# A row-recurrent LSTM after a group normalisation: residual addition to GpSimd three half-steps late, the shared third's normalisation to ScalarE, and a new order in the steady loop

## The chip, the cores and the metric

One Trainium2 chip, one of its cores. The metric is the device time of one execution in microseconds (us), median of several runs. Engines are called as in the profile: PE is TensorE, DVE is VectorE, ACT is ScalarE, POOL is GpSimd, SP is SyncE, which issues all DMAs here.

## The reference

All is float32. `x` is 8 images of 96 channels, 128 rows, 128 columns. It is normalised in 32 groups of three channels; a masked 1x3 convolution makes four gates' inputs for every pixel; then an LSTM runs down the 128 rows, one row at a time, its state passing through a 1x3 convolution along the row; the states are added to `x`.

```python
its = conv(gn(x), W_is * mask) + b_is          # 384 gate rows for each pixel
def step(carry, row_in):
    h, c = carry
    ss = conv1d(h, W_ss) + b_ss                # three taps along the row
    f, i, o, g = split(ss + row_in)            # sigmoid, sigmoid, sigmoid, tanh
    c_new = f * c + i * g
    h_new = o * tanh(c_new)
    return (h_new, c_new), h_new
out = x + scan(step, rows of its)
```

## The kernel before

The rows depend on each other, so the kernel has little else to overlap than two halves of the batch. A half-step is one row of one half (`s`, four images): 96 channels on partitions, 512 pixels along them, even pixels first (`t=0`, 256), then odd ones. `place(n)` gives half-step `n` its row and half: even `n` are half 0, a row ahead. Half-steps 2 to 253 are written by one string of names, `PERIOD`, that `do` plays once for each `n`; the engines then run their instructions in just that order (`manual_schedule`), each waiting on semaphores. A mark behind a name moves it to another half-step: `'` one back, `''` two, `'''` three, `+` one on. `<` and `>` choose the upper or lower 64 rows of TensorE, which work side by side.

The three-tap convolution is done by products of sums and differences. From the new state in `hx` four operands are made: `S` (`total`, L670, `vs`, even plus odd) and `F` (`difference`, L674, `vf`) on DVE, `D0` (`shifted_even`, L680, `te`) and `D1` (`shifted_odd`, L684, `vo`) on POOL. `te` needs only the even pixels of the state, `vo` only the odd ones. The 384 gate rows lie in three PSUM banks of 128 rows: A (forget gate, and 32 rows of g), B (input gate, and 32 rows of o), C (64 rows of o, 64 of g). In each bank products 1 and 2 (with `vs` and `vf`) are made first. ACT copies half of the bank out (`cp`, L583), DVE adds and subtracts (`lo` L587, `hi` L591), and only then products 0 and 3 (with `vo`, `te`) and the products of the input, `P`, `Q` and `E`, are added to the same bank. In the chain of waits, `loC` and `hiC` are the last pair of a half-step, right behind `S` in DVE's queue.

Then come the gates. ACT: `si` (sigmoids, L615; L618 is `o2`, the 32 rows of o in bank B), `ta` (tanh of g, L596), `th` (tanh of the cell, L650, odd pixels then even). DVE: `fg` (f*c, L623), `gtb` (i*g of the odd pixels, L632), `ceb` and `cea` (the cell, L642), `oub` and `oua` (the state, L658). POOL: `gta` (i*g of the even pixels, L630).

Beside the recurrence, POOL prepares later rows: `widen` (L337, `xw`) normalises an image's 64 channels, `add_pixels` (L354) and `subtract_pixels` (L358, `xs`) make the input's operands. In `PERIOD` these are `W1`, `W2` and `W3`. The other 32 channels ("the shared third") share the partitions 96 to 127 of the state's tiles: `normalise_shared` writes them into `hx`, by ACT (L335) where the part is a single row, named `X`, and by POOL (L337, `hx`) otherwise, named `U`. Over four rows each half has four parts of four, four, four and three rows, and one part of one row.

`residual` (`re`) adds the state to the `x` tile in place, on DVE (L700), one half-step behind; then `finish` lets SP store a block of four rows (L703) and, when the store has landed, load the block after next into the same tile (L182, L183).

Of the kernel before, what the change touches and what calls it, by code (L numbers as in the profile page):

```python
# [21 lines left out]
def kernel(  # L22
# [29 lines left out]
    nc = tc.nc  # L52
# [365 lines left out]
    NT = NB * R  # L418
# [3 lines left out]
    def place(n):  # L422

        row, s = divmod(n, NH)
        return row + (LEAD if s == 0 else 0), s
# [50 lines left out]
    class HalfStep:  # L476
# [158 lines left out]
        def part(self, ap, lo, hi, t=None):  # L635
            ap = ap.rearrange("p (t b j) -> p t b j", t=2, b=BH)
            return ap[:, :, lo:hi] if t is None else ap[:, t, lo:hi]
# [52 lines left out]
        def residual(self, lo=0, hi=BH, t=None):  # L690
            s, row = self.s, self.row
            if t is not None:
                xo = xt[s, row // R][0:C, :, row % R, :].rearrange("p b (j t) -> p t b j", t=2)
                nc.vector.tensor_add(xo[:, t], xo[:, t], self.h[:, t])
                return
            xo = xt[s, row // R][0:C, :, row % R, :].rearrange("p b (j t) -> p t b j", t=2)
            if self.n < 1:
                nc.gpsimd.tensor_add(xo, xo, self.h)
            else:
                nc.vector.tensor_add(xo, xo, self.h)  # L700

    def store(s, k, lo, hi):
        nc.sync.dma_start(  # L703
# [40 lines left out]
    def work(n):  # L744
        row, s = place(n)
        if row >= NT:
            return [], (), []
        if n < len(FIRST):
            return FIRST[n]
        k, r = divmod(row, R)  # L750
        ahead, image = (k + 2, 0) if r == R - 1 else (k + 1, r + 1)
        return (
            shared(s, k + 1, *SHARED[r]) if k + 1 < NB else [],
            own(s, ahead, image) if ahead < NB else (),
            ([LATER[n]] if n in LATER else [])
            + ([(spare, s, k + 1)] if r == R - 2 and k + 1 < NB else [])
            + ([(load_rows, s, k + 2)] + ([(load, 0, k + 2)] if s == 1 else [])
               if r == R - 2 and k + 2 < NB else []),
        )
# [3 lines left out]
    def prepare(n, which="123"):  # L763

        channels, image, rest = worked.setdefault(n, [list(parts) for parts in work(n)])
        now = []
        for name, engine in (("X", nc.scalar), ("U", nc.gpsimd)):
            if name in which:
                now += [part for part in channels if part[1] is engine]
                channels[:] = [part for part in channels if part[1] is not engine]  # L770
        for i in "123":
            if i in which and int(i) <= len(image) and image[int(i) - 1]:
                now.append(image[int(i) - 1])
                image[int(i) - 1] = None
        if image.count(None) == len(image) and n not in closed:
            closed.add(n)
            now += rest
        for part, *args in now:
            part(*args)
# [3 lines left out]
    def finish(n):  # L783
        prepare(n)
        row, s = place(n)
        k, r = divmod(row, R)
        if r == R - 1:
            store(s, k, R - 1 if k + 1 == NB else 0, R)
            if s == 1 and k + 2 < NB:
                load(s, k + 2)  # L790
        elif r == R - 2 and k + 1 == NB:
            store(s, k, 0, R - 1)
# [2 lines left out]


    PERIOD = (
        "2B> siA' cpB 2A< siBb' 0C'> 1A< cpA fg' D0'' 3C'> QC< loB QA+> taCb' 1C< hiB PB+> 2C< "
# [3 lines left out]
    )  # L802
    LAST = (
        "2B'' 2A'' 1B'' 1A'' cpB'' cpA'' loB'' 1C'' hiB'' 2C'' loA'' EB'' hiA'' 0B'' 3A'' 0A'' "
        "3B'' cpC'' loC'' EA'' taA'' hiC'' 0C'' 3C'' PA QA PB QB PC QC EA EB siBa'' siA'' siBb'' "
        "fg'' taCb'' taCa'' gtb'' siC'' gta'' ceb'' cea'' o2'' thb'' oub'' tha'' oua'' F'' S'' "
        "D1'' D0'' re'' 1A 2A 1B 1C 2B 2C cpA loA hiA cpB loB 3A hiB 0A 0B 3B cpC loC hiC 0C 3C "
        "taA siA fg o2 siBa siBb taCa taCb gta gtb siC ceb cea thb tha oub oua reb rea"
    )
# [12 lines left out]
    def half_step(n):  # L822
        if n not in steps:
            steps[n] = HalfStep(n)
        return steps[n]

    def do(n, names, by_lanes=False):

        for name in names.split():
            if name in "UX":  # L830
                prepare(n - NH, name)
                continue
            if name[0] == "W":
                prepare(n - 1 + name.count("+") - name.count("'"), name.strip("W+'"))
                continue
            at = n
            for mark, offset in (("'", -1), ("+", 1), ("*", 2)):
                at += offset * name.count(mark)
                name = name.replace(mark, "")
            images = None  # L840
            lane = "<>".find(name[-1]) if name[-1] in "<>" else None
            name = name.rstrip("<>")
            if name[0] in OWN and name[-1] in IMAGES:
                images, full = IMAGES[name[-1]], name[:-1]
            else:
                full = name
            pixels = PIXELS[name[-1]] if name[:-1] in SPLIT and name[-1] in PIXELS else ()
            whole_name = name[:-1] if pixels else full
            tile_ = whole_name[-1] if whole_name[-1] in order else ""
            part = whole_name[: len(whole_name) - len(tile_)]  # L850

            if part in ("S", "F", "D0", "D1"):
                at += NH
            if place(at)[0] >= NT:
                continue
            step = half_step(at)
            if name in step.done or whole_name in step.done:
                continue
            if by_lanes and (part in OWN or part in H_PRODUCTS) and (
                n < last or part in ("P", "Q") or (part, order[tile_]) in step.halves  # L860
            ):
                if step.piece(part, order[tile_], images, lane):
                    step.done.add(name)
                continue
            step.done.add(name)
            getattr(step, PARTS[part])(*([order[tile_]] if tile_ else []), *pixels)
            if by_lanes and part == "re" and at < last:
                finish(at)
# [55 lines left out]
    def next_products():  # L924


        late[0:0] = [Scale(1, 0, BH - 1)]
        late.insert(1, Scale(1, BH - 1, BH, late[0].banks))
        for a in range(2):
            half_step(1).take_bank(a)  # L930
        do(2, "PA PB QA QB PC QC 1A 2A 1B 2B 1C 2C")
# [19 lines left out]
    def keep_warm(count):  # L951
        if not early_done and 1 not in steps:
# [30 lines left out]
        at(4, 10): lambda: (  # L983
            spare_rows(0, 0, 1),
            do(-2, "PA PB QA QB PC QC EA EB"),
        ),
        at(4, 15): lambda: (
            do(-2, "1A 2A 1B 2B 1C 2C"),
            do(-2, "cpA"),
            do(-2, "cpB"),  # L990
# [125 lines left out]
    for b in range(B):  # L1116
# [7 lines left out]
        for k in range(QW // CH):  # L1124
# [11 lines left out]
            if alone:  # L1136
                i = list(shares).index(k)
                part = slice(0, alone * SN) if k % 2 else slice(CH - alone * SN, CH)
# [131 lines left out]
```

## Time and profile before

| | |
|---|---|
| median of 3 runs | 2147.67 us (2146.77 to 2148.72) |
| the profiled execution | 2147.14 us; span of its records 2145.3 us |
| busy: PE, DVE, ACT, POOL | 95%, 86%, 74%, 74% of the span |
| granted TensorE clock | 0.995 of full speed |
| L700 `residual` on DVE | 253 times, 918 ns in the mean, 680 ns at the least |
| L337 `hx`, shared third on POOL | 185 times 869 ns, 60 times 752 ns |
| L335 `hx`, shared third on ACT (one row) | 63 times 493 ns |

How to read it: PE is busy nearly all the time in the records, but a busy record of PE isn't PE at its peak. The steady loop is some 1970 us of the time, so a change of 0.1 us in each half-step is worth 25 us. One query lists instructions by time, with start, duration and, in brackets, the idle time before and what ended it; one follows the chain of work that ended last; one lists least, median and greatest duration of an instruction.

### The profile page before, as it was taken

Reading aid. Unit: us, or ns where it says so; the run is one execution under the profiler, and the core shown is the slowest. Engines: PE = TensorE matmul, PEld = TensorE weight load, DVE = VectorE, ACT = ScalarE, POOL = GpSimd, SP = SyncE. Lnnn points to the kernel's source line nnn. Section 1 sums busy time; section 2 is a strip of 40 time slices with the busy share of each in tenths; the row PEclk is TensorE's granted clock in tenths of the full one; section 3 lists DMA queues with packets and bytes.
Section 4 is the critical chain, followed back from the end, with each engine's and each line's share of the span. In section 5 each row is a group of like instructions: output and inputs, shape, how many; then the busy total and the mean of one; then the engine's idle time right before and its main releaser. Section 6 shows DMA issues by size and latency. Waiting matters only on the chain.

```text
span 2145.3 us, 45095 instructions
## 1 busy us (share of the span) xinstructions
PE 2044.4 (95%) x16400; PEld 1727.8 (81%) x16400; DVE 1841.4 (86%) x4018; ACT 1584.9 (74%) x3519; POOL 1581.3 (74%) x1917
## 2 busy tenths in 40 slices
PE   3689999999999999999999999999999999999998
PEld 0357888888888888888888888888888888888886
DVE  5788888888888888888888888888888888888887
ACT  6687777777777777777777777777777777777776
POOL 4457877777777777777777777777777777777752
PEclk9989999999999999999999999999999999999999
DMA  9973443343344334334433433443343344334311
GB/s 404 412 222 94 99 109 82 95 114 100 84 102 107 84 95 114 99 83 103 107 83 95 114 98 83 104 107 83 95 114 98 83 105 106 83 95 114 92 35 31
DMA packets 110286, 242.79 MB, mean 113 GB/s; under 512 B 6832, under 2 KB 16368, under 8 KB 104048
## 3 DMA queue, kind: packets, MB, share of 16 engines
q1 hardware_dynamic: 110064, 239.89, 42.0%
q8 instruction: 131, 2.15, 0.4%
q14 instruction: 91, 0.75, 0.1%
HBM read 181.34 MB, written 50.33 MB: 108 GB/s over the span
## 4 chain that ended last, share of the span: by engine, by line
DVE 53%; ACT 21%; PE 18%; issue 4%; DMA 2%; POOL 2%; SPq 0%; DVEq 0%; POOLq 0%; ACTq 0%
PE ps L512 18%; DVE ps L591 12%; DVE ps L587 11%; DVE vs L670 9%; ACT ps L650 7%; DVE c L642 7%; ACT m L583 6%; DVE hx L658 5%; DVE vf L674 5%; DVE g L632 3%; ACT g L596 2%; ACT o L618 2%; DMA xs<-in_x_dram 2%; ACT o L615 2%; ACT hx L335 1%
## 5 line engine op out<-in xcount | busy, mean ns | idle before, releaser
L512 PE MATMUL ps<-vo,wl 64*128 64x256 f32 (+1 forms) x3042 | 815.3, 392 | 27.3 <-DVE ps L591 2.1
L512 PE MATMUL ps<-vs,wm 64*128 64x256 f32 (+1 forms) x3046 | 808.2, 397 | 8.4 <-POOL vs L670 6.0
L512 PE MATMUL ps<-vf,wm 64*128 64x256 f32 (+1 forms) x3046 | 794.9, 385 | 3.2 <-DVE vf L674 1.8
L512 PE MATMUL ps<-te,wl 64*128 64x256 f32 (+1 forms) x3042 | 771.7, 377 | 0.0
L512 PE MATMUL ps<-xs,wx 64*128 64x256 f32 (+1 forms) x3080 | 727.7, 377 | 2.0 <-POOL xs L354 1.8
L512 PEld LDWEIGHTS ps<-xs,wx 64*128 64x128 f32 x3080 | 561.4, 187 | 7.4 <-POOL xs L354 3.4
L512 PEld LDWEIGHTS ps<-vo,wl 64*128 64x128 f32 (+1 forms) x3042 | 421.3, 185 | 163.3 <-DVE ps L591 129.4
L512 PEld LDWEIGHTS ps<-vf,wm 64*128 64x128 f32 (+1 forms) x3046 | 492.7, 186 | 71.5 <-DVE vf L674 29.2
L583 ACT ACTIVATE m<-ps,wl 128x256 f32<-128x256 f32 x766 | 363.1, 474 | 235.1 <-PE ps L512 208.9
L596 ACT ACTIVATE g<-ps 32x512 f32<-32x512 f32 x765 | 317.9, 448 | 254.4 <-PE ps L512 247.9
L512 PEld LDWEIGHTS ps<-te,wl 64*128 64x128 f32 (+1 forms) x3042 | 493.0, 187 | 13.3 <-issue 0.2
L512 PEld LDWEIGHTS ps<-vs,wm 64*128 64x128 f32 (+1 forms) x3046 | 424.9, 186 | 67.3 <-DVE vs L670 40.8
L680 POOL TENSOR_TENSOR te<-hx 96x256 f32<-96x256 f32 x254 | 215.4, 848 | 292.8 <-DVE hx L658 290.8
L587 DVE TENSOR_TENSOR ps<-m,ps 128x256 f32<-128x256 f32 x768 | 324.7, 423 | 82.4 <-ACT m L583 82.0
L358 POOL TENSOR_TENSOR xs<-xw 128x512 f32<-128x512 f32 (+1 forms) x254 | 380.5, 1498 | 20.2
L591 DVE TENSOR_TENSOR ps<-m,ps 128x256 f32<-128x256 f32 x768 | 325.8, 425 | 17.6
L658 DVE TENSOR_TENSOR hx<-o,ps 96x256 f32<-96x256 f32 x512 | 197.4, 415 | 130.0 <-ACT ps L650 129.5
L512 PE MATMUL ps<-xs,wt 64*128 64x256 f32 x1012 | 299.4, 376 | 1.5 <-DVE ps L591 1.5
L630 POOL TENSOR_TENSOR g<-i,g 96x256 f32<-96x256 f32 x251 | 182.6, 727 | 123.9 <-ACT g L596 123.9
L615 ACT ACTIVATE ps<-ps 96x512 f32<-96x512 f32 (+1 forms) x512 | 244.0, 477 | 0.2
L700 DVE TENSOR_TENSOR x<-x,hx 96x512 f32<-96x512 f32 x253 | 232.2, 918 | 0.0
L337 POOL TENSOR_SCALAR hx<-x,rstd,nmr 32x512 f32<-32x512 f32 (+1 forms) x245 | 205.8, 840 | 24.7
(118 smaller groups left out, 2524.4 us busy)
## 6 DMA issues: line engine op xcount, KB each, us to landing
xr<-in_x_dram SPq DMA_DIRECT2D x124, 512.0 KB, 6.4
x<-in_x_dram SPq DMA_DIRECT2D x62, 768.0 KB, 5.9
out_dram<-x SPq DMA_DIRECT2D x62, 768.0 KB, 4.7
xs<-in_x_dram SPq DMA_DIRECT2D x31, 1024.0 KB, 11.2
x<-in_x_dram SPq DMA_DIRECT2D x62, 256.0 KB, 3.2
te<-in_x_dram SPq DMA_DIRECT2D x8, 1024.0 KB, 11.3
hx<-in_x_dram SPq DMA_DIRECT2D x8, 1024.0 KB, 9.7
te<-xs SPq DMA_DIRECT2D x62, 128.0 KB, 2.5
```

What stands on the lines that cost most here:

```text
L337: return engine.tensor_scalar(dst, src, scale, shift, ALU.mult, ALU.add)
L358: return engine.tensor_sub(differences, strided(xw[:, 0, :], 0, [(W + 1, n), (J + 1, 2), (1, J)]), strided(xw[:, 0, :], J, [(W + 1, n), (0 ...
L512: made = nc.tensor.matmul(self.ps[a][:, bass.ts(half, HB)][:, cols], weights[rows, bass.ts(a, P)], rhs[rows, cols], start=new, stop=False, ...
L583: nc.scalar.activation(self.m1[a], m1, AF.Identity, bias=column)
L587: nc.vector.tensor_add(self.ps[a][:, 0:HB], self.m1[a], self.ps[a][:, HB:])
L591: nc.vector.tensor_sub(hi, self.m1[a], hi)
L596: nc.scalar.activation(self.part(g, lo, hi, t), self.part(ps, lo, hi, t), AF.Tanh)
L615: nc.scalar.activation(to, gate, AF.Sigmoid)
L658: nc.vector.tensor_mul(self.h[:, t, lo:hi], o, th)
L670: engine.tensor_add(self.operand("vs")[:, 0, lo:hi], e, o)
L680: nc.gpsimd.tensor_sub(to, h[:, :, 1 : J + 1], h[:, :, 0:J])
L700: nc.vector.tensor_add(xo, xo, self.h)
```

## The change

Three edits. `residual` is always given to POOL (L697 in the changed kernel, which is a few lines shorter), and `PERIOD` names it `re'''` instead of `re'`: the state of three half-steps ago. `prepare` now gives the parts of `U` to ACT as well, so that all of the shared third is normalised there. And `PERIOD` and `LAST` have a new order.

```diff
-            if self.n < 1:
-                nc.gpsimd.tensor_add(xo, xo, self.h)
-            else:
-                nc.vector.tensor_add(xo, xo, self.h)
+            nc.gpsimd.tensor_add(xo, xo, self.h)
...
-                now += [part for part in channels if part[1] is engine]
+                now += [
+                    (part[0], nc.scalar, *part[2:]) for part in channels if part[1] is engine
+                ]
...
     PERIOD = (
-        "2B> siA' cpB 2A< siBb' 0C'> 1A< cpA fg' D0'' 3C'> QC< loB QA+> taCb' 1C< hiB PB+> 2C< "
...
+        "2B> 3C'< siBa' D0'' QB+> QC+< 2C> PB+< 1C> loA cpB re''' PC+< hiA 0A> taCb' taCa' loB "
...
-            if place(at)[0] >= NT:
+            if place(at)[0] >= NT or (by_lanes and at < 0):
```

The first place is POOL's queue over one half-step in the middle of the kernel, before: the even operand `te`, the shared third into `hx`, the differences `xs`, the odd operand `vo`, the next image into `xw`, the even product into `g`, the sums `xs`.

```order
L680 TENSOR_TENSOR te0_78<-hx01_71 96x256
L337 TENSOR_SCALAR hx00_70<-x0_16_11221,rstd0_104,nmr0_106 32x4x2x64
L358 TENSOR_TENSOR xs10_76<-xw0_82 128x4x2x64
L684 TENSOR_TENSOR vo_0_63_11758<-hx01_71 128x256
L337 TENSOR_SCALAR xw0_82<-xr0_80,rstd0_104,nmr0_106 128x4x2x64
L630 TENSOR_TENSOR g_1_61_11709<-i_1_61_11723,g_1_61_11709 96x256
L354 TENSOR_TENSOR xs01_75<-xw0_82 128x4x64
```

The same queue now, over as many rows.

```order
L630 TENSOR_TENSOR g_1_61_11600<-i_1_61_11617,g_1_61_11600 96x256
L358 TENSOR_TENSOR xs10_76<-xw0_82 128x4x2x64
L337 TENSOR_SCALAR xw0_82<-xr0_80,rstd0_104,nmr0_106 128x4x2x64
L684 TENSOR_TENSOR vo_1_62_11688<-hx11_73 128x256
L680 TENSOR_TENSOR te1_79<-hx11_73 96x256
L697 TENSOR_TENSOR x0_15_10429<-x0_15_10429,hx01_71 96x2x4x64
L354 TENSOR_TENSOR xs01_75<-xw0_82 128x4x64
```

The shared third is gone from POOL, the residual is new there. Behind the product L630 now stand L358 and L337, and the odd operand L684 comes right behind them and ahead of the even one, L680.

The second place is ACT's queue over one half-step, before, from the copy of bank A of the next half-step to the copy of its bank C, in a half-step whose part `X` is there: `ta`, two sigmoids of o, the two tanhs of the cell and between them the shared third.

```order
L583 ACTIVATE m0_0_73_13514<-ps0_0_73_13434,wl_64 128x256
L596 ACTIVATE g_1_71_13488<-ps2_1_71_13387 64x256 x2
L615 ACTIVATE o_1_71_13535<-ps2_1_71_13387 64x512
L618 ACTIVATE o_1_71_13535<-ps1_1_71_13346 32x512
L650 ACTIVATE ps1_1_71_13346<-c1_85 96x256
L335 ACTIVATE hx01_71<-x0_19_13357,nmr0_106,rstd0_104 32x2x64
L650 ACTIVATE ps2_1_71_13387<-c1_85 96x256
L583 ACTIVATE m2_0_73_13564<-ps2_0_73_13474,wl_64 128x256
```

The same queue now, from the tanh of g in bank A on.

```order
L596 ACTIVATE g_0_67_12390<-ps0_0_67_12280 32x512
L618 ACTIVATE o_0_67_12395<-ps1_0_67_12234 32x512
L583 ACTIVATE m0_1_66_12398<-ps0_1_66_12366,wl_64 128x256
L615 ACTIVATE i_0_67_12407<-ps1_0_67_12234 96x256
L583 ACTIVATE m1_1_66_12419<-ps1_1_66_12324,wl_64 128x256
L596 ACTIVATE g_0_67_12390<-ps2_0_67_12236 64x256 x2
L615 ACTIVATE o_0_67_12395<-ps2_0_67_12236 64x512
L650 ACTIVATE ps1_0_67_12234<-c0_84 96x256
L650 ACTIVATE ps2_0_67_12236<-c0_84 96x256
L335 ACTIVATE hx11_73<-x1_17_12157,nmr1_107,rstd1_105 32x4x2x64
L583 ACTIVATE m2_1_66_12454<-ps2_1_66_12326,wl_64 128x256
```

The sigmoid L618 went from right ahead of the cell's tanhs to ahead of the first copy. The shared third stands behind both tanhs and ahead of the copy of bank C, in each half-step now. The copies L583 come A then B, with one sigmoid between them as before.

The third place is DVE's queue over one half-step from `loC` on, before.

```order
L587 TENSOR_TENSOR ps2_0_69_12762<-m2_0_69_12852,ps2_0_69_12762 128x256
L591 TENSOR_TENSOR ps2_0_69_12762<-m2_0_69_12852,ps2_0_69_12762 128x256
L700 TENSOR_TENSOR x1_16_11454<-x1_16_11454,hx11_73 96x2x4x64
L623 TENSOR_TENSOR ps0_0_69_12722<-ps0_0_69_12722,c0_84 96x512
L587 TENSOR_TENSOR ps1_1_68_12814<-m1_1_68_12886,ps1_1_68_12814 128x256
```

The same now.

```order
L587 TENSOR_TENSOR ps2_0_74_13468<-m2_0_74_13600,ps2_0_74_13468 128x256
L591 TENSOR_TENSOR ps2_0_74_13468<-m2_0_74_13600,ps2_0_74_13468 128x256
L623 TENSOR_TENSOR ps0_0_74_13508<-ps0_0_74_13508,c0_84 96x512
L587 TENSOR_TENSOR ps0_1_73_13598<-m0_1_73_13630,ps0_1_73_13598 128x256
L591 TENSOR_TENSOR ps0_1_73_13598<-m0_1_73_13630,ps0_1_73_13598 128x256
```

The residual is gone; behind `hiC` and `fg` bank A comes ahead of bank B. The rest of DVE's queue has the same instructions in the same order.

More of the change, by code (lines that the diff above doesn't have):

```diff
@@ L797 @@
     PERIOD = (
-        "2B> siA' cpB 2A< siBb' 0C'> 1A< cpA fg' D0'' 3C'> QC< loB QA+> taCb' 1C< hiB PB+> 2C< "
[3 rows of a table removed]
+        "2B> 3C'< siBa' D0'' QB+> QC+< 2C> PB+< 1C> loA cpB re''' PC+< hiA 0A> taCb' taCa' loB "
+        "gtb' 1C< hiB 3A> ceb' 2C< 0B> W2 0A< EB> siC' gta' 3A< 3B> cea' EA< thb' tha' oub' X "
+        "oua' U W3 PA+> cpC 3B< QA+> 0B< F' 2A+> S' 2B+< loC siA siBb W1+ hiC 1A+> 1B+< 0C> 2A+< "
+        "taA D1' 3C> o2 1A+< cpA+ fg 1B+> 0C<"
     )
     LAST = (
-        "2B'' 2A'' 1B'' 1A'' cpB'' cpA'' loB'' 1C'' hiB'' 2C'' loA'' EB'' hiA'' 0B'' 3A'' 0A'' "
-        "3B'' cpC'' loC'' EA'' taA'' hiC'' 0C'' 3C'' PA QA PB QB PC QC EA EB siBa'' siA'' siBb'' "
-        "fg'' taCb'' taCa'' gtb'' siC'' gta'' ceb'' cea'' o2'' thb'' oub'' tha'' oua'' F'' S'' "
+        "re'''' re''' 2A'' 2B'' 1A'' 1B'' cpA'' 2C'' 1C'' loA'' cpB'' hiA'' 0A'' loB'' hiB'' 3A'' 0B'' EB'' "
+        "3B'' EA'' cpC'' loC'' siA'' siBb'' hiC'' 0C'' taA'' 3C'' PA QA PB QB PC QC EA EB o2'' "
+        "fg'' siBa'' taCb'' taCa'' gtb'' ceb'' siC'' gta'' cea'' thb'' tha'' oub'' oua'' F'' S'' "
         "D1'' D0'' re'' 1A 2A 1B 1C 2B 2C cpA loA hiA cpB loB 3A hiB 0A 0B 3B cpC loC hiC 0C 3C "
```

3 rows, old and new, of the table PERIOD are left out of this document.

## The prediction

> **What bounds the kernel now.** I read the page's shares first, then how far apart one instruction of each half-step lies, then the chain of work that ended last, then the queues of ACT, POOL and DVE in order of time.
>
> ```profile
> PE 2044.4 (95%) x16400; PEld 1727.8 (81%) x16400; DVE 1841.4 (86%) x4018; ACT 1584.9 (74%) x3519; POOL 1581.3 (74%) x1917
> ```
> ```profile
> L670 DVE TENSOR_TENSOR vs<-hx x205: 831/834/837, 403.4 to 1999.6; 128x256 f32<-128x256 f32 x103
> ```
>
> 204 half-steps in 1596.2 us: 7.825 us each. The chain shows what they are made of (start, us, what).
>
> ```profile
> 1007.04 0.44 DVE ps L591
> ...
> 1007.52 1.19 PE ps L512 x8
> ...
> 1008.73 0.48 ACT m L583
> ...
> 1011.55 0.43 DVE c L642
> 1011.98 0.68 ACT ps L650 x2
> ...
> 1012.72 0.42 DVE hx L658
> ...
> 1013.16 0.42 DVE vf L674
> 1013.59 0.75 DVE vs L670
> 1014.34 0.35 DVE ps L587
> ...
> 1014.71 0.44 DVE ps L591
> ...
> 1020.05 0.49 ACT hx L335
> ...
> 1020.56 0.39 ACT ps L650
> ...
> 1022.98 0.44 DVE ps L591
> ```
>
> It is one loop per half-step, through all engines. `hiC` (L591) ends at 1007.48 and lets PE go on; four products later (eight records, 1.19) ACT copies a bank, DVE takes it through to the cell (L642), ACT makes the tanhs, DVE the state, F (L674), S (L670), `loC` (L587) and the next `hiC`. From 1007.04 to 1014.71 it is 7.67 us. The next one is 8.27: there ACT's part `X` of the shared third (L335) lies between the two tanhs. Three of one and one of the other make 7.82, as measured. So the residual L700 isn't on the path; DVE does it while PE and ACT turn round.
>
> **Part by part.** I go along this loop.
>
> *The turn-round, 0 to +0.08.* Before, two bank copies with one sigmoid between them; in the new order the same with the banks' names changed. The first starts 1.25 after `hiC`, as before. I take +0.04.
>
> *The tanhs, -0.26.*
>
> ```profile
> 1009.55 0.47 ACT L583 ACTIVATE m<-ps,wl 128x256 f32<-128x256 f32 x1
> 1010.05 0.65 ACT L596 ACTIVATE g<-ps 64x256 f32<-64x256 f32 x2
> ...
> 1011.34 0.59 ACT L618 ACTIVATE o<-ps 32x512 f32<-32x512 f32 x1
> 1011.96 0.69 ACT L650 ACTIVATE ps<-c 96x256 f32<-96x256 f32 x2
> ```
> ```profile
> 1010.78 0.73 POOL L630 TENSOR_TENSOR g<-i,g 96x256 f32<-96x256 f32 x1 [0.34 <-ACT g L596]
> 1011.47 0.73 POOL L354 TENSOR_TENSOR xs<-xw 128x256 f32<-128x256 f32 x1
> 1013.21 0.85 POOL L680 TENSOR_TENSOR te<-hx 96x256 f32<-96x256 f32 x1 [1.01 <-DVE hx L658]
> ```
>
> L596 ends at 1010.70 and the second tanh at 1012.65: 1.95. The first tanh was held by L618 up to 1011.93. With L618 moved ahead of the copies, what stays is POOL's product (starts 0.08 after L596, 0.73), the cell (0.04 and 0.43) and its tanh (0.02 and 0.39): 1.69. That removes 0.26 from each half-step, and in every fourth `X`, 0.60 more, leaves the gap between the tanhs.
>
> *The shared third on ACT: hidden, but for 0.04.*
>
> ```profile
> L700 DVE TENSOR_TENSOR x<-x,hx 96x512 f32<-96x512 f32 x253 | 232.2, 918 | 0.0
> ...
> L335 ACT ACTIVATE hx<-x,nmr,rstd 32x512 f32<-32x512 f32 x7 | 5.9, 843 | 6.9 <-DVE nmr L329 6.7
> ...
> L698 POOL TENSOR_TENSOR x<-x,hx 96x512 f32<-96x512 f32 x2 | 2.6, 1294 | 0.0
> ```
> ```profile
> L337 POOL TENSOR_SCALAR xw<-xr,rstd,nmr x205: 796/808/821, 399.4 to 1995.7; 128x512 f32<-128x512 f32 x103
> ```
>
> It stands between the second tanh and the copy of bank C, for which `loC` waits. After the tanh that takes 0.03 + 0.84 + 0.03 + 0.47 = 1.37, with `X` as well 1.89. `loC` has to wait for S anyway: 0.06 + 0.42 + 0.03 to the start of F, then (next item) 1.31 less an overlap of 0.08, so 1.74. Where `X` is there too, `loC` is 0.17 late, in one half-step of four: 0.04. ACT's work grows from 74% of 7.82 = 5.8 to 6.6 us a half-step, which still fits. If S came earlier, this cover of 0.37 would go first.
>
> *The residual on POOL: no time itself, and 0.92 less on a DVE that wasn't waited for there.* POOL gains 1.29 and loses 0.8; it is busy 5.8 of 7.8 now. L697 stands behind `te`, ahead of the product L630, which waits for ACT anyway.
>
> *F and S against POOL, +0.13: the disputed term.* F and S read two operands in SBUF, and the trace shows such DVE instructions and POOL's as taking turns. Before, POOL was idle when F came; then L680 started 0.05 after F, and S, 0.42 where nothing is beside it, took 0.83, ending 0.28 after L680. F's start to S's end: 1.18. Now L630 waits for the tanh of g, with L358 and L337 right behind it, so POOL is at work when F comes. L630's start to that of its follower is 0.69, L358 takes 1.16, and between L358 and L337 lie 0.11 (below): L337 starts 1.96 after L630. F starts 0.73 + 0.04 + 0.43 + 0.02 + 0.39 + 0.06 + 0.42 + 0.03 = 2.12 after L630. So L337 is 0.16 ahead. POOL first, the prologue:
>
> ```profile
> 162.99 1.16 POOL L358 TENSOR_TENSOR xs<-xw 128x512 f32<-128x512 f32 x1
> 164.26 1.24 POOL L337 TENSOR_SCALAR xw<-xr,rstd,nmr 128x512 f32<-128x512 f32 x1
> ...
> 208.81 0.79 POOL L337 TENSOR_SCALAR xw<-xr,rstd,nmr 128x512 f32<-128x512 f32 x1
> ```
> ```profile
> 164.13 0.42 DVE L674 TENSOR_TENSOR vf<-hx 128x256 f32<-128x256 f32 x1
> 164.47 0.42 DVE L670 TENSOR_TENSOR vs<-hx 128x256 f32<-128x256 f32 x1
> ...
> 209.07 1.08 DVE L700 TENSOR_TENSOR x<-x,hx 96x512 f32<-96x512 f32 x1
> ```
>
> At 164 L337 had started 0.21 ahead of S, and yet S ran in its 0.42 and L337 took 1.24, ending 0.61 after S. At 209 L337 was 0.26 ahead of L700 and went first: L700 took 1.08 instead of its 0.68. So this instruction's start counts for turns only between 0.21 and 0.26 later, and with 0.16 F should still go first. Then L337 waits from before S comes, as L680 did, and goes second: 0.42 + 0.61 + 0.28 = 1.31, +0.13. The bounds are -0.42, if S stays right behind F as at 164 (0.34 + 0.42 = 0.76), and +0.49, if F loses (below).
>
> The Trainium skill (SBUF — State Buffer, "SBUF: two separate sides") says that VectorE and GpSimd share a port pair by an exclusive lock, which whichever of the two starts first keeps for its whole instruction. By the letter of that rule L337 would go first, which is the first rival; S at 164.47 came ahead of an L337 that had started before it, so this trace goes with the lock, but not with the start as printed.
>
> **Sum.** A half-step without `X`: 7.67 + 0.04 - 0.26 + 0.13 = 7.58; with the 0.04, 7.62 in the mean, against 7.825. `PERIOD` writes 252 half-steps, the last four with no image to prepare: 0.205 x 248 = 51 us. The profiled execution took 2147.1 (the median is 2147.7): **2096 us**. About 40 of the 51 come from the half-steps with `X` (8.27 to 7.75, some 62 of them: 32) and 8 or more from the others. Start and end change by little: `LAST` keeps its sequence of products, and a residual of 1.29 there stands ahead of the last row's.
>
> **The rivals.**
>
> *F loses to L337 (slower).* Then F waits out L337 and S the odd operand L684, which now stands ahead of `te`. The last half-steps of this kernel have just that order (POOL: L684, L680):
>
> ```profile
> 2129.62 0.67 DVE L674 TENSOR_TENSOR vf<-hx 128x256 f32<-128x256 f32 x1
> 2130.22 0.83 DVE L670 TENSOR_TENSOR vs<-hx 128x256 f32<-128x256 f32 x1
> ```
> ```profile
> 2129.40 0.62 POOL L684 TENSOR_TENSOR vo<-hx 128x256 f32<-128x256 f32 x1 [1.38 <-DVE hx L658]
> 2129.97 0.80 POOL L680 TENSOR_TENSOR te<-hx 96x256 f32<-96x256 f32 x1
> ```
>
> F ended 0.27 after L684, L680 0.48 after F, S 0.28 after L680. Here: L337's rest 0.80 - 0.16 = 0.64, F 0.27, the POOL operand 0.48, S 0.28: 1.67, +0.49 over 1.18. A half-step is then 7.67 + 0.04 - 0.26 + 0.49 = 7.94, `X` is hidden, +0.115 x 248 = +29: **2176**. It decides where L337's lead passes some 0.21; mine is 0.16 from eight seams read to 0.01 or 0.02. Chance 0.28.
>
> *S stays right behind F (faster still).* The loop falls by 0.55 more, but PE, 95% busy, leaves 5% of 7.825: not under 7.43. 0.39 x 248 = 97: **2050**. Against it: L680 got between F and S in every steady half-step. Chance 0.10.
>
> *The residual's lateness reaches the loads.*
>
> ```profile
> out_dram<-x SPq DMA_DIRECT2D x62, 768.0 KB, 4.7
> ...
> x<-in_x_dram SPq DMA_DIRECT2D x62, 256.0 KB, 3.2
> ```
>
> The block's store comes two half-steps later, and the load of 256 KB, from which ACT makes the shared third, waits for it: 4.7 + 3.2 + 0.1 = 8.0 after the last residual. The first part that reads it comes in the next half-step behind the tanhs, some 10.8 after that residual (7.6, and from about 1.6 to about 4.8 after `hiC`). 2.8 spare; if they were gone, each microsecond costs 62 us, one for each block's load: **2160** with one. Chance 0.05.
>
> *No change* (the gain on the tanhs given back to POOL, about +0.38 in the disputed term): **2143 to 2152**. Chance 0.05. That the change doesn't do what it says is excluded: in the built order L700 and POOL's part of `hx` are gone from the steady loop.
>
> **How the numbers follow.** My case has 0.47: 2096, with 0.08 either way in a half-step 2076 to 2116. Rivals 0.28, 0.10, 0.05, 0.05; 0.05 is left for cases between 2116 and 2143. Faster by over 0.2% (4.3 us, what a measurement of this kernel can just tell): 0.47 + 0.10 + 0.05 = 0.62, and 0.01 for parts of the others: 0.63. Same 0.05. Slower 0.32. The range has to hold my case and the first rival with its own 0.08 upward (2196) and reaches down halfway to the second: 2055 to 2196.
>
> **What would show it.** Right: F at 0.42 and S at about 0.9 in the new trace, L337 `xw` at over 1.1 us, the second tanh ending 1.7 after L596, L335 between tanh and copy with no wait of L587 for L583 but in every fourth half-step. Wrong: F over 0.6 and L337 at 0.81 (first rival); S at 0.42 (second); ACT's L335 waiting for a DMA (third). If L618's move brings less than 0.26, or the first copy starts later than 1.25 after `hiC` because ACT isn't free, the sum fails in that term.

## The result and the profile after

The changed kernel takes 2165.92 us (median of 4, 2164.55 to 2167.02) where the kernel before takes 2147.42 (4 runs) on the same chip: a ratio of 1.0085, 95% interval 1.0068 to 1.0103. It is slower by 18.5 us, inside the range on record but on the other side of no change: the first rival, F losing to L337, is what happened.

The profile after: first the page's busy shares, then the two DVE operands in the steady stretch from 400 to 2000 (least, median and greatest ns).

```profile
PE 2064.0 (95%) x16400; PEld 1716.8 (79%) x16400; DVE 1771.0 (82%) x3765; ACT 1756.3 (81%) x3764; POOL 1589.0 (73%) x1925
```
```profile
L674 DVE TENSOR_TENSOR vf<-hx x202: 608/898/916, 406.1 to 1994.8; 128x256 f32<-128x256 f32 x101
L670 DVE TENSOR_TENSOR vs<-hx x202: 827/829/832, 406.9 to 1995.6; 128x256 f32<-128x256 f32 x101
```

DVE does less than before and ACT more, as the edits say. S starts 202 times from 406.9 to 1995.6: 7.904 each, against 7.825. F takes 0.90 where it took 0.42, and S 0.83 as before. The chain of waits over one half-step (start, us, what):

```profile
1008.83 0.44 DVE ps L591
...
1009.31 1.18 PE ps L512 x8
...
1010.52 0.48 ACT m L583
...
1013.01 0.34 DVE c L642
...
1013.43 0.39 ACT ps L650
...
1013.85 0.39 ACT ps L650
...
1014.26 0.43 DVE hx L658
...
1014.72 0.88 DVE vf L674
1015.60 0.75 DVE vs L670
1016.35 0.35 DVE ps L587
...
1016.72 0.44 DVE ps L591
```

It is the same loop, without L335 in it and without the half-steps of 8.27: the longest from one S to the next is now 8.08. POOL's queue at that time, and ACT's:

```profile
1012.57 0.73 POOL L630 TENSOR_TENSOR g<-i,g 96x256 f32<-96x256 f32 x1 [1.70 <-ACT g L596]
1013.26 1.15 POOL L358 TENSOR_TENSOR xs<-xw 128x512 f32<-128x512 f32 x1
1014.51 0.81 POOL L337 TENSOR_SCALAR xw<-xr,rstd,nmr 128x512 f32<-128x512 f32 x1
1015.28 0.79 POOL L684 TENSOR_TENSOR vo<-hx 128x256 f32<-128x256 f32 x1
1016.03 0.79 POOL L680 TENSOR_TENSOR te<-hx 96x256 f32<-96x256 f32 x1
```
```profile
1011.84 0.65 ACT L596 ACTIVATE g<-ps 64x256 f32<-64x256 f32 x2
...
1014.26 0.73 ACT L335 ACTIVATE hx<-x,nmr,rstd 32x384 f32<-32x384 f32 x1
1015.02 0.48 ACT L583 ACTIVATE m<-ps,wl 128x256 f32<-128x256 f32 x1
```

L337 starts at 1014.51, F at 1014.72. The time by which L337's recorded start is ahead of F's is called its lead from here on. L337 keeps its own 0.81, F ends 0.28 after it, and S 0.28 after L684: so F has waited out L337, and S has waited out L684. From F's start to S's end it is now 1.63, where before it was 1.18. `loC` (L587) comes straight behind S: ACT's copy (ending 1015.50) isn't waited for.

### The profile page after: what moved, and what is told of

It is laid out like the page before. It is cut to its first block, busy times and chain, and to the rows that moved or that the text cites. A ratio compares the mean times of both kernels' runs of the same rounds, so it can differ in the third digit from the quotient of the medians.

```text
span 2165.2 us, 46287 instructions
## 1 busy us (share of the span) xinstructions
PE 2064.0 (95%) x16400; PEld 1716.8 (79%) x16400; DVE 1771.0 (82%) x3765; ACT 1756.3 (81%) x3764; POOL 1589.0 (73%) x1925
## 4 chain that ended last, share of the span: by engine, by line
DVE 59%; PE 17%; ACT 16%; issue 4%; DMA 2%; POOL 1%; ACTq 0%; SPq 0%; DVEq 0%; POOLq 0%
PE ps L512 17%; DVE ps L591 14%; DVE ps L587 13%; DVE vf L674 10%; ACT ps L650 9%; DVE vs L670 9%; ACT m L583 6%; DVE hx L658 5%; DVE g L632 5%; DVE c L642 4%; DMA xs<-in_x_dram 2%; DVE bst L1141 1%; DMA te<-in_x_dram 1%; ACT g L596 0%; POOL xw L337 0%
## 5 line engine op out<-in xcount | busy, mean ns | idle before, releaser
L512 PE MATMUL ps<-vo,wl 64*128 64x256 f32 (+1 forms) x3042 | 889.5, 391 | 27.5 <-DVE ps L591 3.2
L512 PE MATMUL ps<-vf,wm 64*128 64x256 f32 (+1 forms) x3046 | 830.2, 394 | 0.8 <-DVE vf L674 0.8
L512 PE MATMUL ps<-vs,wm 64*128 64x256 f32 (+1 forms) x3046 | 743.3, 395 | 12.1 <-POOL vs L670 8.1
L512 PEld LDWEIGHTS ps<-vo,wl 64*128 64x128 f32 (+1 forms) x3042 | 519.8, 186 | 168.9 <-DVE ps L591 129.6
L583 ACT ACTIVATE m<-ps,wl 128x256 f32<-128x256 f32 x766 | 363.0, 474 | 239.1 <-PE ps L512 212.9
L587 DVE TENSOR_TENSOR ps<-m,ps 128x256 f32<-128x256 f32 x768 | 326.6, 426 | 264.6 <-ACT m L583 264.3
L630 POOL TENSOR_TENSOR g<-i,g 96x256 f32<-96x256 f32 x251 | 182.4, 727 | 441.8 <-ACT g L596 441.8
L512 PEld LDWEIGHTS ps<-vf,wm 64*128 64x128 f32 (+1 forms) x3046 | 444.1, 186 | 17.6 <-DVE vf L674 2.0
L591 DVE TENSOR_TENSOR ps<-m,ps 128x256 f32<-128x256 f32 x768 | 325.6, 424 | 17.5
L697 POOL TENSOR_TENSOR x<-x,hx 96x512 f32<-96x512 f32 x255 | 331.6, 1300 | 0.2 <-DVE hx L658 0.2
L596 ACT ACTIVATE g<-ps 32x512 f32<-32x512 f32 x765 | 317.8, 447 | 13.2 <-PE ps L512 0.9
L358 POOL TENSOR_TENSOR xs<-xw 128x512 f32<-128x512 f32 (+1 forms) x254 | 293.1, 1154 | 0.0
L650 ACT ACTIVATE ps<-c 96x256 f32<-96x256 f32 x512 | 196.0, 383 | 92.6 <-DVE c L642 82.8
L335 ACT ACTIVATE hx<-x,nmr,rstd 32x512 f32<-32x512 f32 (+2 forms) x319 | 240.9, 756 | 15.5 <-DVE nmr L329 6.7
L337 POOL TENSOR_SCALAR xw<-xr,rstd,nmr 128x512 f32<-128x512 f32 (+1 forms) x267 | 211.4, 793 | 36.5 <-DVE nmr L329 11.5
```

The lines of the kernel that those rows point to most:

```text
L335: return engine.activation(dst, src, AF.Identity, bias=shift, scale=scale)
L337: return engine.tensor_scalar(dst, src, scale, shift, ALU.mult, ALU.add)
L358: return engine.tensor_sub(differences, strided(xw[:, 0, :], 0, [(W + 1, n), (J + 1, 2), (1, J)]), strided(xw[:, 0, :], J, [(W + 1, n), (0 ...
L512: made = nc.tensor.matmul(self.ps[a][:, bass.ts(half, HB)][:, cols], weights[rows, bass.ts(a, P)], rhs[rows, cols], start=new, stop=False, ...
L583: nc.scalar.activation(self.m1[a], m1, AF.Identity, bias=column)
L587: nc.vector.tensor_add(self.ps[a][:, 0:HB], self.m1[a], self.ps[a][:, HB:])
```

## The experiments

Theory: L337's lead over F is what costs; take it away, and the rest of the sum on record holds. Rivals: that L618's new place costs more than it brings, that the residual on POOL is what delays things, or that something else sets the 7.90. All are the changed kernel with the edits shown (names of `PERIOD` in the diffs); some build on the run before. Ratios are to the kernel before, run on the same chip (2147.2 to 2147.8).

**L337 behind the operands.**

```diff
-S' 2B+< loC siA siBb W1+ hiC
+S' 2B+< loC siA siBb hiC
...
-D0'' QB+>
+D0'' W1 QB+>
```

> The widening L337 goes behind the two operands of the state on POOL (order L630, L358, odd operand L684, even operand L680, L337, residual L697, L354); all else as in the changed kernel. Turn theory (F waits because L337 is ahead of it by 0.20 us, and the loop now runs through POOL): the odd operand still lies ahead of F, so F waits for it, ends about 0.57 after its start and S about 1.33 after F's start, against 1.63 in the changed kernel; less 0.04 for the half-steps with X: some 0.25 a half-step, about 2104 us. Load theory (the residual's 1.29 us makes POOL too full): the same work on POOL, so within 5 us of 2166. ScalarE theory (the shared third on ACT fills it): within 5 us of 2166.

Measured: 2148.64, ratio 1.0005 (0.9996 to 1.0015): 17 us back of the 62 expected. DVE and POOL in one half-step:

```profile
1014.30 0.59 DVE L674 TENSOR_TENSOR vf<-hx 128x256 f32<-128x256 f32 x1
1014.81 1.06 DVE L670 TENSOR_TENSOR vs<-hx 128x256 f32<-128x256 f32 x1
```
```profile
1014.56 0.79 POOL L680 TENSOR_TENSOR te<-hx 96x256 f32<-96x256 f32 x1
1015.35 1.04 POOL L337 TENSOR_SCALAR xw<-xr,rstd,nmr 128x512 f32<-128x512 f32 x1
```

F still had POOL's odd operand beside it, and S ended 0.52 behind L680, not 0.28. L337 is now right behind L680; whether these 0.24 are its doing is not shown. The time fits none of the expectations, so this run alone decides nothing.

**The even operand first as well, so that POOL is idle when F comes.**

```diff
-S' 2B+< loC siA siBb W1+ hiC
+S' 2B+< loC siA siBb hiC
...
-D0'' QB+>
+D0'' D1'' W1 QB+>
...
-taA D1' 3C>
+taA 3C>
```

> As e1, and the even operand L680, which needs the even half of the state, stands ahead of the odd one again, so that POOL is idle when F starts. Turn theory: F at 0.42, then L680 gets in, S at 0.83 and ending 1.18 after F's start, as before the change: 0.45 less than the changed kernel; loC waits for ACT's copy in the half-steps with X (0.08 in the mean): some 0.37 a half-step, about 2074 us, under both kernels. Load theory and ScalarE theory: within 5 us of 2166.

Measured: 2075.67, ratio 0.9662 (0.9648 to 0.9677).

```profile
1012.75 0.42 DVE L674 TENSOR_TENSOR vf<-hx 128x256 f32<-128x256 f32 x1
1013.09 0.83 DVE L670 TENSOR_TENSOR vs<-hx 128x256 f32<-128x256 f32 x1
1014.21 0.43 DVE L587 TENSOR_TENSOR ps<-m,ps 128x256 f32<-128x256 f32 x1 [0.29 <-ACT m L583]
```
```profile
1012.80 0.85 POOL L680 TENSOR_TENSOR te<-hx 96x256 f32<-96x256 f32 x1 [0.34 <-DVE hx L658]
```

F's start to S's end is 1.17, as before the change, so the disputed term is at nothing. The 0.29 in front of L587 is in a half-step with `X`, late at ACT: with S this early the cover is used up there, as the prediction said. The other terms give 7.67 + 0.04 - 0.26 = 7.45, and 0.07 more for this wait in one half-step of four: 7.52. Measured are 71.5 us less, 0.288 a half-step: 7.54. This tests the sum of those terms, not each of them.

**The residual back on DVE, right behind `hiC`.**

```diff
-            nc.gpsimd.tensor_add(xo, xo, self.h)
+            if self.n < 1:
+                nc.gpsimd.tensor_add(xo, xo, self.h)
+            else:
+                nc.vector.tensor_add(xo, xo, self.h)
...
-cpB re''' PC+<
+cpB PC+<
...
-hiC 1A+>
+hiC re' 1A+>
```

> The changed kernel with the residual back on DVE, one half-step late, right behind hiC; order of the rest and the shared third on ACT as changed. Turn theory: the residual's place on POOL is behind both operands and ahead of an idle time, so it costs nothing there and its return brings nothing: 2166 within 6 us, F still 0.9 us. Load theory: POOL's new 1.29 us is the cause, so the time falls under the 2147 of the kernel before, to about 2100.

Measured: 2162.64, ratio 1.0065 (1.0050 to 1.0080), F at 0.89. Where the residual is done makes 3 us, so the residual's load on POOL is not the cause.

**L618 back ahead of the tanhs.**

```diff
-siC' gta'
+siC' o2' gta'
...
-3C> o2 1A+<
+3C> 1A+<
```

> The changed kernel with the sigmoid L618 back at its old place, between the sigmoid of bank C and the tanhs of the cell. Turn theory: the second tanh ends 0.3 later, but F waits for the end of L337 anyway, which depends on POOL's product L630 and not on the tanhs; F's wait shrinks by as much and the time stays: 2166 to 2178 (up to 0.05 a half-step, where X makes the copy of bank C late). Additive theory (the terms of the sum add up one by one, the tanhs' 0.2 was a true gain): 0.2 to 0.3 a half-step more, 2215 to 2240.

Measured: 2176.27, ratio 1.0127 (1.0110 to 1.0144). F comes later and now waits less for the same L337:

```profile
1017.53 0.81 POOL L337 TENSOR_SCALAR xw<-xr,rstd,nmr 128x512 f32<-128x512 f32 x1
```
```profile
1017.96 0.65 DVE L674 TENSOR_TENSOR vf<-hx 128x256 f32<-128x256 f32 x1
```

Undoing L618's move costs 10 us, not 0.26 a half-step (64 us): most of what ACT gains there is given back while F waits for L337. In both kernels the loop runs through POOL: L630, L358, L337, F.

**Memsets of an unused tile between L358 and L337.** They are there to move L337's start alone; a control for that comes below. (The kernels with memsets have a line or more on top: F is L675, S L671, L337 L338, L684 L685.) Three, and eight:

```diff
+                for _ in range(3 if i == "1" and 10 < n < 250 else 0):
+                    nc.gpsimd.memset(pad, 0.0)
                 now.append(image[int(i) - 1])
```

> The changed kernel, with three memsets of 128x4 on POOL between L358 and L337 of each half-step. In the changed kernel L337 starts 0.20 ahead of F; the prologue of before shows such memsets 0.04 apart, so L337 should start some 0.12 later and its lead be some 0.08. Theory now (whichever instruction is first, by the record's start, goes first): F still loses, waits 0.12 less (0.78 instead of 0.90), but L337 ends 0.12 later, and with it L684 and S: 0.12 more in a half-step, 8.02, 2166 + 30 = 2196. The reading on record (L337's start counts only from some 0.21 on): F goes first at 0.42 and S ends 1.31 after F's start, a half-step of 7.58: 2104.

> As the one before, with eight memsets: L337 should start some 0.32 later than in the changed kernel, 0.12 behind F. Both theories: F goes first at 0.42 and L337 takes over 1.1. Then the sum on record for the rest of the term holds: F 0.42, L337's run 0.61, S 0.28 after it, 1.31 in all against the 1.64 of the changed kernel, so 0.33 less in a half-step: 2166 - 82 = 2084 to 2104. If the start of L337 by itself takes a turn, as the run with W1 behind the operands left open (S 0.24 longer there), 0.24 goes again: 2145.

Measured: 2044.31, ratio 0.9519 (0.9505 to 0.9534), and 2042.13, ratio 0.9507 (0.9491 to 0.9523). With three:

```profile
1014.63 0.43 DVE L675 TENSOR_TENSOR vf<-hx 128x256 f32<-128x256 f32 x1
1014.98 0.42 DVE L671 TENSOR_TENSOR vs<-hx 128x256 f32<-128x256 f32 x1
```
```profile
1014.67 1.33 POOL L338 TENSOR_SCALAR xw<-xr,rstd,nmr 128x512 f32<-128x512 f32 x1
```

L337 starts 0.04 behind F, not 0.08 ahead as meant, and does not even get in between F and S: it waits for both and ends 0.60 after S. F's start to S's end is 0.77. That is the second rival on record (2050). The expectations of both runs were too high, since they had L337 ahead of F or between F and S.

Two memsets:

> As the run with three memsets between L358 and L337, with two. There the three took 0.41, began 0.05 ahead of L358's end, and L337 started 0.34 behind that end, 0.04 behind F, and lost; in the changed kernel it starts 0.10 behind L358's end, 0.20 ahead of F, and wins. Two should put it some 0.07 to 0.10 ahead of F. Theory A (the first by the record's start goes first): F loses, L337 ends some 0.12 later than in the changed kernel, the half-step grows by as much: some 2195. Theory B (the reading on record, L337's start counts only some 0.21 later): F goes first, S right behind it, as with three: 2044. The run tells on which side of 0.1 the border lies.

Measured: 2088.22, ratio 0.9722 (0.9706 to 0.9739).

```profile
1011.16 0.42 DVE L675 TENSOR_TENSOR vf<-hx 128x256 f32<-128x256 f32 x1
1011.50 0.89 DVE L671 TENSOR_TENSOR vs<-hx 128x256 f32<-128x256 f32 x1
```
```profile
1011.04 1.07 POOL L338 TENSOR_SCALAR xw<-xr,rstd,nmr 128x512 f32<-128x512 f32 x1
```

The time lies between the two expectations. L337 starts 0.12 ahead and F still goes first; L337 comes in between, S ends 0.28 after it, 1.23 from F's start. This is the very course that the prediction gave to the changed kernel (1.31, 2096).

One memset, long or short, to find the border:

> As the runs with memsets between L358 and L337, with one memset of 128x100. At a lead of 0.12 of L337's start over F's (two memsets) F went first, at 0.20 (the changed kernel) it lost. One longer memset should start L337 some 0.14 behind L358's end instead of 0.10 and 0.18: a lead of 0.16, just what the prediction had read. Theory A (the lead was mis-read, the border lies above 0.16): F 0.42, S 0.89, the half-step as with two memsets, 2088. Theory B (the border itself was mis-read, it lies between 0.12 and 0.16): F loses, waits 0.04 less than in the changed kernel, and S ends 0.04 later: 2166 + 10 = 2176.

> One memset of 128x4 between L358 and L337, the control: it ends before L337 may start (0.10 behind L358's end), so the lead should stay 0.20. If only the lead counts: F loses as in the changed kernel, 2166. If a memset in that place by itself lets F go first: 2044 to 2090.

> The run with one memset of 128x100 left L337 0.19 ahead of F (the memset took 0.18 and L337 started 0.02 before its end, 0.10 behind L358's), and F lost. One of 128x145 should take 0.04 more and put the lead at some 0.16. Theory A (the prediction's lead was mis-read, the border lies above 0.16): F 0.42, S 0.89, 2088. Theory B (its border was mis-read, below 0.16): F loses, 2170.

> As the one before, with a memset of 128x170: a lead of some 0.14. Theory A (border above 0.16): F first, 2088. Theory B: F first as well if the border lies between 0.14 and 0.16, or else F loses, 2172.

Measured: 2168.18 (1.0097, 1.0082 to 1.0112), 2163.39 (1.0073, 1.0057 to 1.0090), 2173.40 (1.0123, 1.0106 to 1.0140) and 2177.61 (1.0140, 1.0125 to 1.0155). The first missed its mark: its lead was to be 0.16 and stayed at 0.19. The second is the control: one memset there with the lead kept leaves F at 892 ns, and the time 2.5 us from that of the changed kernel. The last one:

```profile
1017.40 0.24 POOL L774 MEMSET pad<- 128x170 f32 x1
1017.62 0.79 POOL L338 TENSOR_SCALAR xw<-xr,rstd,nmr 128x512 f32<-128x512 f32 x1
```
```profile
1017.75 0.94 DVE L675 TENSOR_TENSOR vf<-hx 128x256 f32<-128x256 f32 x1
```

L337 0.13 ahead, and F loses. All of them in order of L337's lead (medians over the half-steps from 400 to 2000; lead and F's start to S's end in us, F and S in ns):

| kernel | L337 ahead of F | F | S | F start to S end | time, us |
|---|---|---|---|---|---|
| L618 back | 0.43 | 653 | 829 | 1.40 | 2176.3 |
| the changed kernel | 0.19 | 898 | 829 | 1.65 | 2165.9 |
| one memset, 128x4 | 0.19 | 892 | 829 | 1.64 | 2163.4 |
| one, 128x100 | 0.19 | 898 | 829 | 1.65 | 2168.2 |
| one, 128x145 | 0.15 | 924 | 829 | 1.68 | 2173.4 |
| one, 128x170 | 0.13 | 949 | 829 | 1.70 | 2177.6 |
| two, 128x4 | 0.12 | 425 | 884 | 1.23 | 2088.2 |
| three | -0.04 | 426 | 419 | 0.76 | 2044.3 |
| eight | -0.83 | 425 | 419 | 0.76 | 2042.1 |

Between the kernel at 0.13 and the one at 0.12 there is a step of 89 us. From 0.19 down to 0.13 a smaller lead only makes things worse, since L337 ends later and F still waits for it.

The lead alone doesn't place this step to a hundredth, though. These two kernels differ in more: the one has a single long memset ahead of L337, the other two short ones, and their leads vary a little from half-step to half-step and overlap. One half-step of the first, then one of the second:

```profile
1853.36 0.79 POOL L338 TENSOR_SCALAR xw<-xr,rstd,nmr 128x512 f32<-128x512 f32 x1
1853.47 0.95 DVE L675 TENSOR_TENSOR vf<-hx 128x256 f32<-128x256 f32 x1
```
```profile
586.33 1.07 POOL L338 TENSOR_SCALAR xw<-xr,rstd,nmr 128x512 f32<-128x512 f32 x1
586.46 0.42 DVE L675 TENSOR_TENSOR vf<-hx 128x256 f32<-128x256 f32 x1
```

At leads from 0.120 to 0.128 F lost in all 44 half-steps of the kernel with one memset, and went first in all 130 of the kernel with two. Above 0.13 F lost to L337 in every kernel of the table, and below 0.12 it went ahead of it in every one. What decides in the hundredth between is not shown.

**What gets in between F and S?** With the even operand first, L680 at 0.05 behind F does; L337 at 0.04 behind F doesn't. Either it is the instruction, or that L680 came out of idleness. Three memsets ahead of L680 in that kernel (in `shifted_even`):

```diff
+                for _ in range(3 if 10 < self.n < 250 else 0):
+                    nc.gpsimd.memset(pad, 0.0)
                 nc.gpsimd.tensor_sub(to, h[:, :, 1 : J + 1], h[:, :, 0:J])
```

> The run with the even operand first and W1 behind the operands (2075.7; L680 starts 0.05 behind F and gets in between F and S, S 0.83), with three memsets on POOL ahead of L680. L680 then starts at about the same time, 0.34 behind L358's end, but directly behind POOL's own work instead of out of idleness. With three memsets L337 at 0.04 behind F did not get in between (S 0.42). Theory A (it is the kind of instruction: L680 gets in between F and S, L337 does not): S 0.83, 2076. Theory B (it is where it comes from: behind work of its own engine it does not get in): S 0.42, 0.41 less in a half-step, down to where TensorE's products set the end, 2044 to 2050.

Measured: 2071.39, ratio 0.9645 (0.9630 to 0.9659), and in between it gets:

```profile
1017.83 0.85 POOL L683 TENSOR_TENSOR te<-hx 96x256 f32<-96x256 f32 x1
```
```profile
1017.78 0.42 DVE L675 TENSOR_TENSOR vf<-hx 128x256 f32<-128x256 f32 x1
1018.12 0.84 DVE L671 TENSOR_TENSOR vs<-hx 128x256 f32<-128x256 f32 x1
```

So L680 need not come out of idleness to get in. Next, the changed kernel with the residual in L337's place behind four memsets, and L337 where the residual was:

```diff
-siBb W1+ hiC
+siBb re'' hiC
...
-D0'' QB+>
+D0'' W1 QB+>
...
-cpB re''' PC+<
+cpB PC+<
```

> The changed kernel with the residual (L697 there, two half-steps late instead of three) in the place of L337 behind L358, with four memsets between, and L337 behind the operands where the residual was. The residual should start 0 to 0.1 behind F. It has two operands in SBUF, as L680, and no semaphore to wait for. Theory A (it is the kind of instruction): it gets in between F and S, as L680 did; S then takes 0.4 + 1.2, F's start to S's end some 1.9 instead of the 0.77 with three memsets, and the half-step is 1.1 longer than there: some 2310. Theory B (an instruction behind its own engine's work does not get in between): S 0.42; the operands then come 0.6 later than with three memsets, which costs nothing to 0.6 a half-step: 2044 to 2190.

Measured: 2354.11, ratio 1.0962 (1.0946 to 1.0978).

```profile
1014.97 1.41 POOL L700 TENSOR_TENSOR x<-x,hx 96x512 f32<-96x512 f32 x1
1016.35 0.61 POOL L685 TENSOR_TENSOR vo<-hx 128x256 f32<-128x256 f32 x1
```
```profile
1014.80 0.42 DVE L675 TENSOR_TENSOR vf<-hx 128x256 f32<-128x256 f32 x1
1015.15 2.08 DVE L671 TENSOR_TENSOR vs<-hx 128x256 f32<-128x256 f32 x1
```

The residual (here L700) gets in between though it starts 0.17 behind F. So both POOL operations on two tensors that were tried get in, and L337, a normalisation of one tensor by two scalars, doesn't from 0.04 behind. S ends 0.27 after L685, not after L700: it lost two turns, and the time is above the expected 2310.

**Who keeps the turn?** L337 behind the residual, so that the residual follows L680 at once; then with one 128x4 memset between L680 and the residual:

```diff
-siBb W1+ hiC
+siBb hiC
...
-cpB re''' PC+<
+cpB re''' W1 PC+<
```

> The changed kernel with L337 behind the residual L697, so that POOL's row is L630, L358, L684, L680, L697, L337, L354. It differs from the run with W1 behind the operands (2148.6) in what follows L680 at once: there L337, which has a semaphore to wait for, here L697, which in the order has none. Theory A (a POOL instruction that follows at once without a wait keeps the turn from the waiting S, as L358 behind L680 did at 206.92 in the prologue of before, where S took 1.95): S takes about 1.06 + 1.0, the half-step grows by about 1.0, 2400. Theory B (the 0.24 that S lost in the other run is L337's own): S at 0.83, 0.24 less in a half-step, 2148.6 - 60 = 2089. Theory C (any follower costs 0.24): 2149.

> The run with W1 behind the residual (2389.6; L697 follows L680 at once and S waits for both, 2.08), with one memset of 128x4 between L680 and L697. Theory A (the gap decides: an instruction that follows without a gap keeps the turn; the memset opens one): S ends some 0.3 to 0.5 behind L680, F's start to S's end 1.33 to 1.57, 2100 to 2150. Theory B (the memset is such a follower itself, or L697 is taken ahead of S all the same): S at 2.0 or more, 2390 or above.

Measured: 2389.64, ratio 1.1126 (1.1110 to 1.1143), and 2397.76, ratio 1.1164 (1.1147 to 1.1180). The first:

```profile
1012.62 0.79 POOL L680 TENSOR_TENSOR te<-hx 96x256 f32<-96x256 f32 x1
1013.37 1.28 POOL L697 TENSOR_TENSOR x<-x,hx 96x512 f32<-96x512 f32 x1
```
```profile
1012.86 2.08 DVE L670 TENSOR_TENSOR vs<-hx 128x256 f32<-128x256 f32 x1
```

S waits from 1012.86, and yet POOL goes from L680 to the residual ahead of it: a waiting DVE instruction can be passed over. The time is what was expected if a follower with no semaphore to wait for keeps the turn. But the run before speaks against that cause: L685 does wait for semaphores in the order, and went ahead of S as well. In the second run the memset gave S no turn; it took 2.12. What decides it stays open.

**The best of them.** `X` moved behind L618, where ACT waits for PE, first in the kernel with the even operand first (`X+` is the part of one half-step on):

```diff
-oub' X oua'
+oub' oua'
...
-o2 1A+<
+o2 X+ 1A+<
```

> The run with W1 behind the operands and the even operand first (2075.7), with the part X of the shared third moved one place on ACT: from behind the tanhs to behind L618, where ACT waits 0.35 to 0.45 for PE. In a quarter of the half-steps loC no longer waits 0.29 for ACT's copy: 0.07 in the mean, 18 in all, 2058. If X behind L618 holds the next copy by 0.1 or 0.15 in those half-steps: 2064 to 2067. If something else ends as late as that copy: 2075.

Measured: 2121.86, ratio 0.9882 (0.9868 to 0.9897): 46 us slower than without it.

```profile
1029.39 0.49 ACT L335 ACTIVATE hx<-x,nmr,rstd 32x128 f32<-32x128 f32 x1 [1.82 <-DMA x<-in_x_dram]
```

That is the third rival's mechanism, brought about: the block's load, held back by the late residual, isn't there yet. ACT waits for it 60 times, 77.5 us in all. So with three memsets, `X` in this place, and the residual a half-step earlier (`re''`):

> The run with three memsets (2044.3), with X moved behind L618 and the residual one half-step earlier (re'' for re'''), since in the run with X behind L618 ACT waited 1.3 for the block's load in each of 60 half-steps, 77 in all. With three memsets the half-steps with X take some 0.5 more than the others (loC waits 0.70 for ACT). Theory: the load now lands 7.3 earlier, ACT doesn't wait for it, and X takes 0.49 where ACT waits 0.28 for PE: some 0.3 less in 62 half-steps, 2026. If the load is still late: 2044 to 2120. If PE's own products set the time there: 2044.

Measured: 2015.80, ratio 0.9388 (0.9374 to 0.9402), 10 us better than expected, and ACT's shared third no longer waits for the load. It beats the kernel before by 132 us and the changed kernel by 150.

## Why the prediction was wrong

*The turn-round (0 to +0.08, taken +0.04): right.* From the end of L591 (1009.27) to the end of the second copy it is 2.54, as before.

*The tanhs (-0.26): right in kind, a little short.* From L596's end (1012.49) to the second tanh's end (1014.24) it is 1.75, not 1.69: -0.20. The first tanh starts 0.09 behind its cell, and the second follows the first.

*The shared third on ACT, and the residual: right.* Both are hidden. `X` leaving the loop brings its 0.15 a half-step; in the changed kernel S comes so late that the 0.04 isn't paid. (By its own terms `loC` was to be 0.15 late with `X`, 1.89 less 1.74, and not 0.17; a quarter of it is 0.04 all the same.)

*F and S against POOL (+0.13): the step that failed.* It is +0.45 (1.63 less 1.18), against 0.49 for the first rival. 7.67 + 0 - 0.20 + 0.45 is 7.92, less 0.03 between the tanh and F: 7.89, as the half-step shown has it (1008.83 to 1016.72). The mean is 7.904.

The step rested on two readings. The lead of L337, on record 0.16, was 0.19 in the median, and 0.21 in the half-step shown: there L337 started 0.02 sooner behind L630 (1.94) and F 0.03 later (2.15). And the border, the lead from which F loses, on record between 0.21 and 0.26, lies at 0.12 to 0.13. Only the second decided: at a lead of 0.15, F lost too. It came from one row read against the wrong partner. At 164 L337 had started 0.21 ahead of S and S went first; but S followed F, and L337 had started 0.13 *behind* F. The runs show that L337 behind F by 0.04 doesn't get in between the two, so that row can't tell of a delay before L337's start counts. L700 at 209, which lost at 0.26, fits the border measured; nothing between it and zero had been seen, and the forecast needed just that stretch.

The Trainium skill (SBUF — State Buffer, "SBUF: two separate sides") has the first to start keep the port pair for its whole instruction; by that rule F would lose, as it did. The runs agree above a lead of 0.13. In the kernel with two memsets L337 starts 0.12 ahead by the record, and F goes first all the same.

*The rivals.* The first decided, with its price within 0.04 in a half-step (2176 against 2165.9). The second did not occur here, but three memsets, which put L337's start behind F's, bring it about, at 2044. Its floor of 7.43, from PE being busy for 95% of 7.825, was no floor: the best run makes 7.29 a half-step (218 starts of S from 404.6 to 1986.4). There PE's 16400 records are busy for 1939.5 us, and before for 2044.4, so its busy time is not a fixed amount of work. The third did not occur here, and its spare of 2.8 was about right: `X` was placed some 4.7 earlier (in the half-step above, L618 ends at 1009.59 and the second tanh at 1014.24) and waited 1.3 in the mean, which leaves an estimated 3.4.

*What was not tried:* one long memset against two short ones at the same lead on either side of the border, which would tell what else than the lead counts there; and the changed kernel with L337's scalars held in another form, which might tell why it doesn't get in between F and S where an operation on two tensors does.

## What to carry to other kernels

Where DVE and POOL both work from SBUF, look at which instruction of the one starts just ahead of a critical instruction of the other: starting L337 some 0.23 later, from 0.19 ahead of F to 0.04 behind it, took 5.6% off the time here (2165.9 to 2044.3), and three memsets on POOL were enough for it. When a forecast hangs on such an order, a row that shows it counts only if it has the same pair, with the same predecessor; a border read between two other pairs isn't a border. And a cover that hides a piece of work (here the load behind the residual) is to be worked out again for each place that the work is moved to.

## What the runs showed of the hardware

- Of F and L337, L337 went first at every lead above 0.13, up to the 0.43 of the kernel with L618 back, and F at every lead below 0.12. The change is a step: F's median is 949 ns in the kernel at 0.13 and 425 in the one at 0.12. Leads from 0.120 to 0.128 occur in both and went either way, by kernel.
- Two DVE instructions back to back kept the turn over a waiting L337 that started 0.04 behind the first (S 419 ns, L337 1.33 us), but not over the two POOL operations on two tensors that were tried: L680 0.05 behind F and the residual 0.17 behind F got in between (S 834 and 2087 ns).
- A waiting DVE instruction can lose more than one turn: S took 2.08 with the residual behind L680, 2.12 with a memset between them. When POOL passes it over and when not (behind L680, L684 let it in) is not settled.
- A memset of 128x4 on POOL takes 0.10 alone, and two in a row take 0.25, three 0.41.
